# Three edits to a graph-and-experts kernel: how sources are counted, how in-degrees are turned, and which expert results are put by

## The chip, the cores and the metric

The kernel runs on one core of a Trainium2 chip. Its engines are TensorE (PE in the profile, with PEld for its weight loads), VectorE (DVE), ScalarE (ACT), GpSimd (POOL) and SyncE (SP, which here issues transfers only). Each engine works through its own queue in order; semaphores tie them together. Transfers run on 16 DMA engines, whichever engine issued them. The metric is the device time of one execution in microseconds. Nine runs of the kernel before have a median of 1886.43 us (1877.25 to 1897.92).

## The reference

6250 nodes with 256 features, 106,250 directed edges sorted by destination, and eight experts of which each node uses two:

```python
x = x + gnn(layernorm(x), src, dst, W, b)
x = x + ffn(layernorm(x), Wr, br, ln_g, ln_b, W1, b1, W2, b2)

def gnn(f, src, dst, W, b):
    out_deg, in_deg = segment_sum(ones, src), segment_sum(ones, dst)
    msg = (f @ W)[src] * rsqrt(max(out_deg, 1))[src][:, None]
    return relu(segment_sum(msg, dst) * rsqrt(max(in_deg, 1))[:, None] + b)

def ffn(x, ...):
    top_p, top_idx = top_k(softmax(x @ Wr + br), 2)
    weights = top_p / top_p.sum(-1)
    h = gelu((norm(x) * ln_g[e] + ln_b[e]) @ W1[e] + b1[e])    # for each expert e
    y = h @ W2[e] + b2[e]
    return (weights * y of the two chosen experts).sum()
```

Out-degrees are needed before any message can be scaled; in-degrees only when a node's sum is complete.

## The kernel before

**First stage: counting and scaling (about the first 147 us).** The nodes' rows sit in `xres` as 49 tiles of 128. The out-degree of every node is counted by matmuls: a node's number is split into two digits (`digits`, L357), the low one of 7 bits (128 values) and the high one of 49 values. The 106,250 sources lie as 128 rows of 831 columns; `counts` (L367) takes them in 26 chunks of 32 columns. For each chunk DVE makes two one-hot blocks, `oh_hi` (49 x 32, L370) and `oh_lo` (128 x 32, L375), by comparing the digits with counting patterns that GpSimd wrote (`steps_of`, L317 and L318), and PE runs one matmul for each column (L381, 831 in all) that adds into the PSUM tile `hist` (128 x 49), so that node t x 128 + p stands at row p, column t. The blocks have two buffers each. Meanwhile ACT sums the rows and their squares (L465, L475) and copies the turned lists of sources and destinations (L400), which PE turns (L397) behind the chunks of the count that are ahead of it in its queue. The degrees (L515), then scale and shift, multiply the rows of `xres`, which go out to a table `ytab`. The first 42 messages are gathered from x itself and scaled by the degrees of their own sources, for which the digits of those 42 columns are taken too (L408) and turned into one-hots (L415 to L427).

**Second stage: gathers.** A loop over 831 chunks of 128 edges (L1345). For each, POOL issues one indirect DMA (`gather`, L1262), 24 chunks ahead of its use, which fetches 128 rows from `ytab`, or from chunk 168 on from `ptab`, the same table as three bf16 parts. PE multiplies the messages by a one-hot of the destinations (L1372, or the three matmuls L1375 to L1377) into `pm`. The 257th column of a message is 1, so the last column of `pm` counts in-degrees. After a batch of 14 chunks `finish` (L731) turns the sums by PE, two blocks of 128 features with transposes (L741) and the degree column with a matmul by the identity that repeats it over 128 rows (L742), and DVE adds all three blocks into a window of `ring` (L747). When a tile of 128 nodes is complete, `tile_sums` (L773) multiplies it by W (L781), turns its degrees back into a column with a matmul against a one (L785), and finishes the rows; these are stored to the output (L807), and `route_group` sends the normalized rows, sorted by expert, to a table `xs` (POOL scatters, L965).

**Expert steps.** One step takes 256 rows (128 in the first eight steps) of one expert: SyncE loads the rows `xin` and the expert's weights `w` (L1131, L1136; 2182 KB, two buffers), PE turns the rows (L1144), multiplies by W1 (L1201) and W2 (L1220), ACT applies gelu (L1210), and DVE adds the bias and multiplies by the gate into `yo` (L1231, L1237), which has three buffers. The result is added to the output by POOL with two indirect DMAs that accumulate (`add_up`, L1093, line L1095 in the profile). The two adds of one step may overlap (`declare_no_dep`); adds of different steps write the same output and wait for one another. Steps run among the chunks of the second stage as soon as an expert has rows enough, and the remaining ones after the last chunk: the tail.

**Results put by.** While the gathers run (`deferring`, until the loop reaches chunk 807), every third full step is not added to the output at once: `put_by` (L1173) stores its `yo` to a table `ys` by SyncE during the next step, which also frees the buffer. At the end of the gathers `take_back` (L1104) loads them again, up to four at a time, into message buffers, and `add_back` (L1114) adds one step's result to the output, twice in the last chunks and then once in 16 turns of the tail's loop ("beats", L1407 to L1425; about 17 beats are one step, and there are 281 in all):

```python
if sb == SB and deferring[0] and done[0] % 3 == 0:
    stores.append((yo, to_i))
```

**Order.** The program fixes the order of PE, DVE, ACT and SP by hand throughout, and that of POOL until chunk 807; from there on POOL's instructions are placed by the scheduler.

Of the kernel before, what the change touches and what calls it, by code (L numbers as in the profile page):

```python
# [18 lines left out]
P = 128  # L19
# [4 lines left out]
def gnn_then_moe(  # L24
# [12 lines left out]
    nc = tc.nc  # L37
    N, D = x.shape
    NE = src.shape[0]
    E = wr.shape[1]  # L40
    KD = D // P
# [4 lines left out]
    NT = -(-N // P)  # L46
# [18 lines left out]
    WIN = P  # L65
# [5 lines left out]
    GC = 32  # L71
    LO = P
    NHI = NT
    NCP = -(-NCH // GC) * GC
    MW = D + 4
    NMSG = 42
# [4 lines left out]
    SB = TB // P  # L81
# [35 lines left out]
    for g in range(len(GS) - 1):  # L117
        n = P * sum(GS[: g + 1])
# [7 lines left out]
    n = P * sum(GS[:-1])  # L126
# [110 lines left out]
    with tc.manual_schedule(), tc.tile_pool(  # L237
        name="hl", bufs=1
    ) as hl, tc.tile_pool(
        name="rows", bufs=1  # L240
# [7 lines left out]
        flat = hl.tile([P, NCP], I32, name="src_flat")  # L248
        lo = hl.tile([P, NCP], BF16, name="src_lo")
        hi = hl.tile([P, NCP], BF16, name="src_hi")  # L250
        iota_lo = hl.tile([P, LO, GC], BF16, name="iota_lo")
        iota_hi = hl.tile([P, NHI, GC], BF16, name="iota_hi")
        zeros = const.tile([P, SB * XW], F32, name="zeros")
        if FULL < NCP:
            nc.vector.memset(flat[:, FULL:NCP], NPAD - 1)
# [61 lines left out]
        steps_of(iota_hi, [[1, NHI], [0, GC]])  # L317
        steps_of(iota_lo, [[1, LO], [0, GC]])  # L318
        ident = const.tile([P, P], F32, name="ident")
        make_identity(nc, ident)  # L320
        pcol = const.tile([P, 1], F32, name="pcol")
        steps_of(pcol, [[0, 1]], 0, 1)
        steps_of(iota_w, [[1, WIN]])
        for i in range(NMSG):
            nc.gpsimd.memset(msg[i][:, D : D + 1], 1.0)
        after = const.tile([P, P], F32, name="after")
# [27 lines left out]
                in_offset=bass.IndirectOffsetOnAxis(ap=firstT[:, i : i + 1], axis=0),  # L354
            )

        def digits(v, lo, hi, n):  # L357
            for op, by, to in ((ALU.bitwise_and, LO - 1, lo), (ALU.logical_shift_right, 7, hi)):
                part = rows.tile([P, NCP], I32, tag="part", name="part")[:, :n]
                nc.vector.tensor_scalar(part, v, by, None, op0=op)  # L360
                nc.vector.tensor_copy(to, part)

        digits(flat, lo, hi, NCP)
        hist = s1h.tile([P, NT], F32, name="hist")
        chunks = iter(starts)

        def counts(m):  # L367
            for _, c0 in zip(range(m), chunks):
                oh_hi = s1o.tile([P, NHI, GC], BF16, tag="oh_hi", name="oh_hi")
                nc.vector.tensor_tensor(  # L370
                    oh_hi, iota_hi,
                    hi[:, None, c0 : c0 + GC].to_broadcast([P, NHI, GC]), ALU.is_equal,
                )
                oh_lo = s1o.tile([P, LO, GC], BF16, tag="oh_lo", name="oh_lo")
                nc.vector.tensor_tensor(  # L375
                    oh_lo, iota_lo,
                    lo[:, None, c0 : c0 + GC].to_broadcast([P, LO, GC]), ALU.is_equal,
                )
                n = min(GC, NCH - c0)
                for c in range(n):  # L380
                    nc.tensor.matmul(  # L381
                        hist, oh_lo[:, :, c], oh_hi[:, :, c],
                        start=(c0 + c == 0), stop=(c0 + c == NCH - 1),
                    )
# [23 lines left out]
        digits(firstT, lo_e, hi_e, NMSG)  # L408
        loT = rows.tile([P, NMSG, P], BF16, name="loT")
        ohe_hi = rows.tile([P, NMSG, NHI], BF16, name="ohe_hi")  # L410
        nc.vector.tensor_tensor(
            ohe_hi, iota_w[:, None, :NHI].to_broadcast([P, NMSG, NHI]),
            hi_e[:, :, None].to_broadcast([P, NMSG, NHI]), ALU.is_equal,
        )
        for c0 in range(0, NMSG, GC):  # L415
            n = min(GC, NMSG - c0)
            oh_lo = s1o.tile([P, LO, GC], BF16, tag="oh_lo", name="oh_lo")
            nc.vector.tensor_tensor(
                oh_lo[:, :, :n], iota_lo[:, :, :n],
                lo_e[:, None, c0 : c0 + n].to_broadcast([P, LO, n]), ALU.is_equal,  # L420
            )
# [90 lines left out]
        nc.vector.tensor_scalar(sqs, sqs, 1.0 / D, None, op0=ALU.mult)  # L512
        rs0 = rsqrt(rows, sqs, NT, "rs0", EPS)
        deg = rows.tile([P, NT], F32, name="deg")
        nc.vector.tensor_scalar(deg, hist, 1.0, None, op0=ALU.max)  # L515
        both = rows.tile([P, 2, NT], F32, name="both")
        scale0, shift0 = both[:, 0, :], both[:, 1, :]
        nc.vector.tensor_tensor(scale0, rsqrt(rows, deg, NT, "ns"), rs0, ALU.mult)
# [212 lines left out]
    def finish(b, pm):  # L731

        s = seg(b)
        ag = s3.tile([P, D + 1], F32, tag="ag", name="ag")
        nc.scalar.copy(ag, pm)
        if b and seg(b - 1) < s:
            nc.vector.tensor_copy(ring[s][:, :, :OVER], ring[s - 1][:, :, SEGN:])
        yield 0.0, 2
        pt = psum()[:, : (KD + 1) * P].rearrange("p (k q) -> p k q", q=P)
        for k in range(KD):  # L740
            nc.tensor.transpose(pt[:, k, :], ag[:, k * P : (k + 1) * P], ident)  # L741
        nc.tensor.matmul(  # L742
            pt[:, KD, :], ag[:, D : D + 1].to_broadcast([P, P]), ident,
            start=True, stop=True,
        )
        w = register(mybir.EngineType.DVE, win_i[0:1, b : b + 1], RING - WIN)
        nc.vector.tensor_tensor(  # L747
            ring[s][:, :, bass.ds(w, WIN)], ring[s][:, :, bass.ds(w, WIN)], pt, ALU.add
        )
        for t in range(NT):  # L750
            if CLOSE[t] == b:
                side.append([now[0] + 2, 1, tile_sums(t, ring[s], t * P - SEGN * s)])
        yield 0.7, 1
# [19 lines left out]
    def tile_sums(t, sums, c0):  # L773

        g, i = place[t]
        if i == 0:
            held[g] = s3.tile([P, GMAX, 2], F32, tag="mv1", name="mv1")
        x2, mv1 = x_of[t], held[g]
        pw = psum()
        for k in range(KD):  # L780
            nc.tensor.matmul(  # L781
                pw[:, :D], sums[:, k, c0 : c0 + P], gw_sb[:, k, :],
                start=(k == 0), stop=(k == KD - 1),
            )
# [338 lines left out]
    def expert_steps(todo, forever):  # L1123
# [58 lines left out]
        while True:  # L1182
# [224 lines left out]
    while side or todo or batches or not pace["idle"]:  # L1407
        now[0] += 1
        run_side(1.2)
        if batches:  # L1410
            batch = batches.pop(0)
            if batch[0] == len(GS) - 1:
                final = batch
                todo.extend((batch, n) for n in range(PARTS[0]))
            else:
                todo.extend((batch, n) for n in range(STEPS[batch[0]]))
        run_steps(0.9)
        for _, one in rows_out + sums_out:
# [76 lines left out]
```

## Time and profile before

| | |
|---|---|
| median of 9 runs | 1886.43 us |
| profiled execution, its own time | 1898.08 us |
| its span, first to last instruction | 1896.4 us |
| granted TensorE clock, mean | 0.874 |
| PE busy | 1438.2 us (76%) |
| POOL busy | 1147.8 us (61%) |
| DVE busy | 874.8 us (46%) |
| ACT busy | 393.8 us (21%) |
| last gather issued / last result written by DVE / last instruction | 1575.0 / 1882.9 / 1885.4 us |
| `hist` matmuls L381 | 831, 85.4 us busy |
| scatter-adds from `yo` / from `msgs` (results put by) | 86 / 18 |
| stores to `ys` | 9 of 256 KB |

How to read it: the span is cut by stage, since shares over the whole of it mix limits. "Idle before, releaser" tells how long an engine stood idle ahead of a group of instructions and what ended most of that; an engine's idle time costs nothing unless the engine is the one that others wait for. POOL's busy time for an indirect DMA is the time it takes to write its descriptors; the data lands later. Between the last instruction and the end of the span the last add lands and the program closes.

### The profile page before, as it was taken

How to read it: one execution, taken by the hardware profiler on the slowest of the kernel's cores; microseconds unless marked ns; L12 is line 12 of the kernel's file. 1: busy time of each engine (PE TensorE's matmuls, PEld its weight loads, DVE VectorE, ACT ScalarE, POOL GpSimd, SP SyncE). 2: the span in 40 equal slices, each digit the busy share in tenths (PEclk: the TensorE clock that was granted, in tenths of full speed). 3: DMA queues.
4: the chain of work that ended last, by engine and by line, in shares of the span. 5: the costliest groups of instructions: out<-in, count | busy, mean ns of one | idle time of the engine just before them, and what ended most of it. 6: DMA issues, size and time to landing. Idle time of an engine off the chain costs nothing. (4 is left out here: it accounts for less than half of the span.)

```text
span 1896.4 us, 23690 instructions
## 1 busy us (share of the span) xinstructions
PE 1438.2 (76%) x7890; PEld 1171.4 (62%) x7890; DVE 874.8 (46%) x3123; ACT 393.8 (21%) x978; POOL 1147.8 (61%) x1127
## 2 busy tenths in 40 slices
PE   6964645556666797777778878787799699799996
PEld 5863533445555676655556657566577587678886
DVE  8992555425244273444524535426246354722211
ACT  3661211002011120210202112112112112322221
POOL 8847756466757667576666666765766573432321
PEclk9997767678778898898788889898899899899999
DMA  7736756277566776667567577666677576586773
GB/s 223 267 118 231 230 163 192 84 268 241 181 210 202 271 231 209 215 185 231 176 223 207 183 237 222 219 213 197 206 234 253 169 239 204 153 250 188 206 214 72
DMA packets 146583, 389.50 MB, mean 205 GB/s; under 512 B 22316, under 2 KB 89364, under 8 KB 139282
## 3 DMA queue, kind: packets, MB, share of 16 engines
q0 software_dynamic: 70176, 179.11, 34.2%
q1 hardware_dynamic: 76218, 208.73, 31.0%
q8 instruction: 66, 1.08, 0.2%
q14 instruction: 67, 0.55, 0.1%
q10 hardware_dynamic: 56, 0.02, 0.0%
HBM read 324.26 MB, written 63.52 MB: 204 GB/s over the span
## 5 line engine op out<-in xcount | busy, mean ns | idle before, releaser
L1271 POOL DMA_INDIRECT msgs<-ptab,srcT x663 | 649.6, 980 | 332.1 <-issue 131.4
L1201 PE MATMUL ph<-xeT,w 128*128 128x256 f32 (+1 forms) x1792 | 466.0, 398 | 125.0 <-issue 70.3
L1201 PEld LDWEIGHTS ph<-xeT,w 128*128 128x128 f32 x1792 | 339.0, 211 | 176.8 <-issue 79.6
L1220 PE MATMUL py<-w,hT 128*128 128x256 f32 x1664 | 428.3, 392 | 10.9 <-issue 9.3
L1210 ACT ACTIVATE hT<-ph,w 128x256 f32<-128x256 f32 (+1 forms) x448 | 179.8, 455 | 845.8 <-PE ph L1201 371.1
L1220 PEld LDWEIGHTS py<-w,hT 128*128 128x128 f32 x1664 | 304.4, 197 | 47.4 <-issue 11.4
L1095 POOL DMA_INDIRECT out_x<-yo,to_all x86 | 137.7, 1601 | 187.2 <-DVE yo L1237 50.5
L1375 PE MATMUL pm<-msgs,oh 128*128 128x257 bf16 x663 | 193.0, 291 | 4.4 <-issue 4.4
L1376 PE MATMUL pm<-msgs,oh 128*128 128x256 bf16 x663 | 191.6, 289 | 6.0 <-issue 5.9
L1377 PE MATMUL pm<-msgs,oh 128*128 128x256 bf16 x663 | 190.9, 288 | 4.7 <-issue 4.5
L1149 DVE TENSOR_SCALAR xeT<-ptf,w 128x256 f32<-128x256 f32 (+1 forms) x112 | 53.5, 520 | 301.5 <-PE ptf L1144 123.9
L1271 POOL DMA_INDIRECT msgs<-ytab,srcT x126 | 125.7, 998 | 57.9 <-issue 29.1
L747 DVE TENSOR_TENSOR ring<-ring,misc 128x384 f32 x60 | 33.2, 554 | 253.4 <-PE pm L1377 85.4
L223 DVE TENSOR_TENSOR oh<-iota_w,relT 128x896 bf16<-128x896 f32 (+2 forms) x119 | 128.0, 1080 | 24.5 <-remote 10.6
L965 POOL DMA_INDIRECT xs<-rowt,pos_i x98 | 100.8, 1029 | 61.3 <-issue 47.2
L781 PE MATMUL misc<-gw_sb,ring 128*128 128x256 f32 x196 | 64.7, 460 | 74.3 <-DVE ring L747 37.5
L1376 PEld LDWEIGHTS <-oh 128*128 128x128 bf16 x663 | 69.0, 104 | 73.1 <-issue 17.3
L1372 PE MATMUL pm<-msgs,oh 128*128 128x257 f32 x336 | 101.8, 458 | 9.4 <-PEq L576 4.3
L781 PEld LDWEIGHTS misc<-gw_sb,ring 128*128 128x128 f32 x196 | 39.5, 223 | 88.3 <-DVE ring L747 41.4
L381 PE MATMUL hist<-oh_hi,oh_lo 128*128 128x49 bf16 x831 | 85.4, 279 | 11.3 <-DVE oh_lo L375 10.8
L381 PEld LDWEIGHTS <-oh_lo 128*128 128x128 bf16 x831 | 82.4, 150 | 14.2 <-DVE oh_lo L375 13.5
L1372 PEld LDWEIGHTS pm<-msgs,oh 128*128 128x128 f32 x336 | 74.9, 234 | 22.5 <-ACTq L576 4.4
(600 smaller groups left out, 1590.4 us busy)
## 6 DMA issues: line engine op xcount, KB each, us to landing
w<-in_wcat SPq DMA_DIRECT2D x56, 2182.0 KB
xin<-xs SPq DMA_DIRECT2D x48, 260.0 KB
msgs<-ptab,srcT POOLq DMA_INDIRECT x663
strayT<-zeros SPq DMA_DIRECT2D x1, 9216.0 KB
ptab<-part SPq DMA_DIRECT2D x24, 384.0 KB
ytab<-xres SPq DMA_DIRECT2D x7, 896.0 KB
ring<-strayT SPq DMA_DIRECT2D x4, 1536.0 KB
x<-in_x SPq DMA_DIRECT2D x48, 128.0 KB
```

Source lines behind the costliest of these rows:

```text
L223: nc.vector.tensor_tensor(oh[:, :n, :], iota_w[:, None, :].to_broadcast([P, n, WIN]), relT[:, c : c + n, None].to_broadcast([P, n, WIN]), ...
L381: nc.tensor.matmul(hist, oh_lo[:, :, c], oh_hi[:, :, c], start=(c0 + c == 0), stop=(c0 + c == NCH - 1),)
L781: nc.tensor.matmul(pw[:, :D], sums[:, k, c0 : c0 + P], gw_sb[:, k, :], start=(k == 0), stop=(k == KD - 1),)
L1095: ad = nc.gpsimd.indirect_dma_start(out=out, out_offset=bass.IndirectOffsetOnAxis(ap=to, axis=0), in_=rows, in_offset=None, compute_op=ALU ...
L1201: nc.tensor.matmul(ph[:, c - c0, :tb], w[:, k * H + c * P : k * H + (c + 1) * P], xeT[:, k, :tb], start=(k == 0), stop=(k == KD - 1),)
L1210: nc.scalar.activation(hT[:, c, :tb], ph[:, c - c0, :tb], AF.Gelu, bias=w[:, OB1 + c : OB1 + c + 1],)
L1220: nc.tensor.matmul(py[:, s, :], hT[:, c, s * P : (s + 1) * P], w[:, OW2 + c * D : OW2 + (c + 1) * D], start=(c == 0), stop=(c == HC - 1),)
L1271: nc.gpsimd.indirect_dma_start(out=to, out_offset=None, in_=table, in_offset=bass.IndirectOffsetOnAxis(ap=srcT[:, c : c + 1], axis=0),)
L1372: nc.tensor.matmul(pm, oh, msg[i % NMSG][:, : D + 1], start=first, stop=last)
L1375: nc.tensor.matmul(pm, oh, part[:, PW - D : PW + 1], start=first, stop=False)
L1376: nc.tensor.matmul(pm[:, :D], oh, part[:, D : PW - D], start=False, stop=False)
L1377: nc.tensor.matmul(pm[:, :D], oh, part[:, :D], start=False, stop=last)
```

## The change

Three edits. (1) The source count splits a node's number into a low digit of 6 bits (64 values) and a high one of 98. The one-hot blocks become 64 x 32 and 98 x 32, `hist` becomes 64 x 98, and two DVE instructions bring it back to 128 x 49. The 42 early columns keep 7 bits and get a counting pattern of their own, `iota_e`, in blocks of 16 columns. (2) In `finish` the degree column is turned with a transpose into one row in place of 128 equal ones, and DVE's add is split into one for the features (128 rows) and one for that row; in `tile_sums` a transpose takes the place of the matmul by a one. (3) While edges are gathered, the results of two full steps in three are put by, in place of one in three, and in the tail's loop one is added back in 14 beats in place of 16.

```diff
+    CLO, CHI = P // 2, 2 * NT
+    GE = GC // 2
...
-        iota_lo = hl.tile([P, LO, GC], BF16, name="iota_lo")
-        iota_hi = hl.tile([P, NHI, GC], BF16, name="iota_hi")
+        iota_lo = hl.tile([P, CLO, GC], BF16, name="iota_lo")
+        iota_hi = hl.tile([P, CHI, GC], BF16, name="iota_hi")
+        iota_e = hl.tile([P, LO, GE], BF16, name="iota_e")
...
+        steps_of(iota_e, [[1, LO], [0, GE]])
...
-        digits(flat, lo, hi, NCP)
-        hist = s1h.tile([P, NT], F32, name="hist")
+        digits(flat, lo, hi, NCP, CLO)
+        hist = s1h.tile([CLO, CHI], F32, name="hist")
...
-                oh_hi = s1o.tile([P, NHI, GC], BF16, tag="oh_hi", name="oh_hi")
+                oh_hi = s1o.tile([P, CHI, GC], BF16, tag="oh_hi", name="oh_hi")
...
-                oh_lo = s1o.tile([P, LO, GC], BF16, tag="oh_lo", name="oh_lo")
+                oh_lo = s1o.tile([P, CLO, GC], BF16, tag="oh_lo", name="oh_lo")
...
-        for c0 in range(0, NMSG, GC):
-            n = min(GC, NMSG - c0)
-            oh_lo = s1o.tile([P, LO, GC], BF16, tag="oh_lo", name="oh_lo")
+        for c0 in range(0, NMSG, GE):
+            n = min(GE, NMSG - c0)
+            oh_lo = s1o.tile([P, LO, GE], BF16, tag="oh_lo", name="oh_lo")
...
-        nc.vector.tensor_scalar(deg, hist, 1.0, None, op0=ALU.max)
+        for h in range(2):
+            nc.vector.tensor_scalar(
+                deg[h * CLO : (h + 1) * CLO, :], hist[:, h:CHI:2], 1.0, None, op0=ALU.max
+            )
...
-        nc.tensor.matmul(
-            pt[:, KD, :], ag[:, D : D + 1].to_broadcast([P, P]), ident,
-            start=True, stop=True,
-        )
+        nc.tensor.transpose(pt[0:1, KD, :], ag[:, D : D + 1], ident)
...
-        nc.vector.tensor_tensor(
-            ring[s][:, :, bass.ds(w, WIN)], ring[s][:, :, bass.ds(w, WIN)], pt, ALU.add
-        )
+        for rows, ks in ((P, slice(0, KD)), (1, slice(KD, KD + 1))):
+            place_of = ring[s][:rows, ks, bass.ds(w, WIN)]
+            nc.vector.tensor_tensor(place_of, place_of, pt[:rows, ks, :], ALU.add)
...
-        nc.tensor.matmul(
-            pw[:, D : D + 1], sums[0:1, KD, c0 : c0 + P], ones[0:1, 0:1],
-            start=True, stop=True,
+        nc.tensor.transpose(
+            pw[:, D : D + 1], sums[0:1, KD, c0 : c0 + P], ident[0:1, 0:1]
         )
...
-            if sb == SB and deferring[0] and done[0] % 3 == 0:
+            if sb == SB and deferring[0] and done[0] % 3:
                 stores.append((yo, to_i))
...
-        if beat % 16 == 8:
+        if beat % 14 == 6:
             add_back()
```

More of the change, by code (lines that the diff above doesn't have):

```diff
@@ L315, in steps_of @@
                            allow_small_or_imprecise_dtypes=True)
-        steps_of(iota_hi, [[1, NHI], [0, GC]])
-        steps_of(iota_lo, [[1, LO], [0, GC]])
+        steps_of(iota_hi, [[1, CHI], [0, GC]])
+        steps_of(iota_lo, [[1, CLO], [0, GC]])
         ident = const.tile([P, P], F32, name="ident")
@@ L355, in gnn_then_moe, with digits @@
             )
-        def digits(v, lo, hi, n):
-            for op, by, to in ((ALU.bitwise_and, LO - 1, lo), (ALU.logical_shift_right, 7, hi)):
+        def digits(v, lo, hi, n, base):
+            for op, by, to in (
+                (ALU.bitwise_and, base - 1, lo),
+                (ALU.logical_shift_right, base.bit_length() - 1, hi),
+            ):
                 part = rows.tile([P, NCP], I32, tag="part", name="part")[:, :n]
@@ L368, in counts @@
             for _, c0 in zip(range(m), chunks):
-                oh_hi = s1o.tile([P, NHI, GC], BF16, tag="oh_hi", name="oh_hi")
+                oh_hi = s1o.tile([P, CHI, GC], BF16, tag="oh_hi", name="oh_hi")
                 nc.vector.tensor_tensor(
                     oh_hi, iota_hi,
-                    hi[:, None, c0 : c0 + GC].to_broadcast([P, NHI, GC]), ALU.is_equal,
+                    hi[:, None, c0 : c0 + GC].to_broadcast([P, CHI, GC]), ALU.is_equal,
                 )
-                oh_lo = s1o.tile([P, LO, GC], BF16, tag="oh_lo", name="oh_lo")
+                oh_lo = s1o.tile([P, CLO, GC], BF16, tag="oh_lo", name="oh_lo")
                 nc.vector.tensor_tensor(
                     oh_lo, iota_lo,
-                    lo[:, None, c0 : c0 + GC].to_broadcast([P, LO, GC]), ALU.is_equal,
+                    lo[:, None, c0 : c0 + GC].to_broadcast([P, CLO, GC]), ALU.is_equal,
                 )
@@ L407, in gnn_then_moe @@
         hi_e = rows.tile([P, NMSG], F32, name="hi_e")
-        digits(firstT, lo_e, hi_e, NMSG)
+        digits(firstT, lo_e, hi_e, NMSG, LO)
         loT = rows.tile([P, NMSG, P], BF16, name="loT")
@@ L414, in gnn_then_moe @@
         )
-        for c0 in range(0, NMSG, GC):
-            n = min(GC, NMSG - c0)
-            oh_lo = s1o.tile([P, LO, GC], BF16, tag="oh_lo", name="oh_lo")
+        for c0 in range(0, NMSG, GE):
+            n = min(GE, NMSG - c0)
+            oh_lo = s1o.tile([P, LO, GE], BF16, tag="oh_lo", name="oh_lo")
             nc.vector.tensor_tensor(
-                oh_lo[:, :, :n], iota_lo[:, :, :n],
+                oh_lo[:, :, :n], iota_e[:, :, :n],
                 lo_e[:, None, c0 : c0 + n].to_broadcast([P, LO, n]), ALU.is_equal,
```

## The prediction

> **What bounds the kernel now.** I read the windows of time first, to tell the stages apart, then the groups of instructions, then the timelines of GpSimd (POOL) and SyncE in the last stage and of PE, DVE and ACT in the first. The chain of waits was no help: it holds one piece, the last DMA. In a window line the columns are its length, then busy us (and instructions) of PE, weight load, DVE, ACT and POOL, the granted clock, the DMA share and GB/s.
>
> ```profile
> 1200.00:1300.00 100.00, 79.65 (x430) 61.92 (x429) 36.68 (x123) 14.01 (x33) 67.05 (x66) 0.91 0.67 208
> 1700.00:1800.00 100.00, 100.00 (x479) 88.06 (x478) 21.53 (x70) 23.47 (x56) 31.13 (x21) 1.00 0.69 203
> ```
>
> There are three stages: until about 147 us a first one, in which degrees are counted; the gathers, whose last POOL issue is at 1575 us; then a tail in which PE does nothing but expert steps and is never idle. While edges are gathered, neither PE nor POOL is full, so the next question is who waits for whom.
>
> ```profile
> L1271 POOL DMA_INDIRECT msgs<-ptab,srcT x663 | 649.6, 980 | 332.1 <-issue 131.4
> L1095 POOL DMA_INDIRECT out_x<-yo,to_all x86 | 137.7, 1601 | 187.2 <-DVE yo L1237 50.5
> L1375 PE MATMUL pm<-msgs,oh 128*128 128x257 bf16 x663 | 193.0, 291 | 4.4 <-issue 4.4
> ```
>
> The third line decides: ahead of the 663 matmuls that first touch a gathered message PE idles 4.4 us in all. Messages are never late. The table of waits says the reverse: POOL waits 109.5 us (134 times) for PE to release a message buffer. So POOL's time between 150 and 1575 us is not on the path, PE's order of work is, with its waits on DVE and ACT. The tail looks PE-bound, but its scatter-adds into the output tell another story (POOL's timeline, first add of most pairs, and SyncE's for the same stretch):
>
> ```profile
> 1737.44 1.55 POOL L1095 DMA_INDIRECT out_x<-yo,to_all  x1 [8.34 <-DVE xeT L1149]
> 1739.30 1.55 POOL L1095 DMA_INDIRECT out_x<-yo,to_all  x1 [0.31 <-issue]
> 1743.87 1.55 POOL L1095 DMA_INDIRECT out_x<-msgs,to_all  x1 [3.02 <-issue]
> ...
> 1771.40 1.55 POOL L1095 DMA_INDIRECT out_x<-yo,to_all  x1 [3.04 <-DMA out_x<-msgs,to_all]
> ...
> 1781.22 1.55 POOL L1095 DMA_INDIRECT out_x<-yo,to_all  x1 [6.42 <-DVE gate L1170]
> ...
> 1793.73 1.55 POOL L1095 DMA_INDIRECT out_x<-yo,to_all  x1 [9.11 <-DMA out_x<-yo,to_all]
> ...
> 1799.94 1.55 POOL L1095 DMA_INDIRECT out_x<-yo,to_all  x1 [2.81 <-DMA out_x<-yo,to_all]
> ```
> ```profile
> 1769.39 0.33 SPq L1136 DMA_DIRECT2D w<-in_wcat  x1
> ...
> 1783.65 0.33 SPq L1136 DMA_DIRECT2D w<-in_wcat  x1
> ```
>
> Two adds make a pair, one step's result. A pair starts only when the pair before it has landed. Pair starts run 1737.4, 1743.9, 1752.7, 1765.0, 1771.4, 1781.2, 1793.7, 1799.9, 1809.3, 1822.2, 1828.5: ten distances in 91.1 us, 9.1 us each, in a pattern of about 6.4, 9.4 and 12.6 us, which sums to two steps (weight loads leave SyncE every 14.25 us). The short ones have no weight load behind them; the long ones do, so an add lands late while 2182 KB of weights pass. I write this as **6.4 us for each pair and 4.65 us more for each weight load**: 3 x 6.4 + 2 x 4.65 = 28.5. POOL is busy only 31 of 100 us there, yet this chain of landings has no room: counted back from the last step, the pairs at 1781.2 and 1793.7 carry results that DVE began to write at 1755.1 and 1769.3, some 24 us late. The chain catches up only near 1841, with one pair a step.
>
> **Part 1, put by two of three.** 48 full steps run, 29 of them before results stop being put by (at chunk 807 of 831; the loops' own counts put the 29th at chunk 798 and the 30th at 813). Now 9 go to ys (9 stores in the list of DMAs); then 29 - 9 = 20. Eleven pairs leave the gather stage and come back in the tail.
> What it gives in the gather stage: 22 adds x (1.60 + 0.30 gap) = 42 us of POOL. I take **0** of it, since PE idles 4.4 us for messages; the ends are 0 and 42. What it adds there: 11 stores of 256 KB on SyncE, 0.33 us of issue each, queued behind the next step's weight load and waiting for a result that is done by then; 2.8 MB at 205 GB/s is 14 us of DMA in a stage with a share of 0.6 to 0.75. Hidden by that free share; without it weights come late, up to 14 us.
> In the tail: before, 20 step pairs and 9 put by; after, 19 and 20, so 39. Slots: two at the end of the gathers, then a beat in 14 from 6 on, 18 slots up to beat 244 of 281, so nothing is left over for the drain. From the first slot (1639.5 us, once POOL has sent the last rows to xs) there are 18 put-by pairs and 17 step pairs, and 15 weight loads. The last pair starts 34 x 6.4 + 15 x 4.65 = 287 us after the first. The same count on the kernel before, from 1639.5 to 1841.2, has 20 distances and 13 loads, 188 us, and 9 us in which the chain waited for results: 197, against 201.7 measured. So I add 4 us: 291. Last pair at 1930.5 in place of 1883.5: **+47 us**. The next thing late is DVE's result write: yo has three buffers, released by the adds, so steps are held back and PE idles about 4 us a step (2.2 x 6.4 + 4.65 = 18.7 us of chain, 14.25 us of work). Ends: with no delay by weights at all 34 x 6.4 = 218, ready at 1857, no loss (0); with 9.1 us for each pair 309, +65. Twenty-two more loads of 128 KB from ys use a DMA share of 0.31 that is free.
> The Trainium skill, TensorE: Matmul & The Clock Gate (Part 1), has the clock halve after some 3.4 us of idle PE. The row that bears on it is the window 300 to 400 us, PE busy 45.66 with 0.67 granted, against 1.00 above. By the page each held-back step starts at half clock and would lose an estimated 1.7 us; that lies inside the idle time and alters nothing in my sum.
>
> **Part 2, the source count.**
>
> ```profile
> 109.20 6.40 PE L381 MATMUL hist<-oh_hi,oh_lo 128*128 128x49 bf16 x63 [0.19 <-DVE oh_lo L375]
> ...
> 124.66 2.45 PE L556 MATMUL pk<-part,loT 128*128 128x98 bf16 x28 [0.38 <-DVE part L525]
> ```
> ```profile
> 80.84 0.65 ACT L400 CAST srcT<-ptE 128x240 int32<-128x240 f32 x1 [14.38 <-PE ptE L397]
> ```
> ```profile
> 114.00 1.09 DVE L223 TENSOR_TENSOR oh<-iota_w,relT 128x896 f32<-128x896 f32 x1 [1.76 <-ACT relT L400]
> ```
>
> DVE makes two one-hots a chunk: 2286 ns for 4096 elements, 971 for 1568, so 0.520 ns an element and 155 fixed. After: 2048 and 3136 elements, 1220 + 1787 = 3007 against 3257, 0.25 us less. ACT waits 14.4 us for PE's first turned rows at 80.8, behind 16 chunks, and is then back to back to 114, where DVE waits for it. So only the 16 chunks count: 4.0 us, about 1.2 for DVE's short waits on PE (0.2 to 0.4 each), 1.0 for a shorter last chunk on PE, less 0.2 for a second DVE pass over the histogram: **-6 us**, between -3 and -9. GpSimd's iotas: 1673 + 4169 ns become 3.2 + 2.15, and 2.15 more ahead of 42 gathers; POOL waits 23.2 us for DVE later, which hides it. The edges' one-hots cost 0.2 us more.
> On PE a chunk's matmul, now 128 weight columns and 49 moving, both strided, goes every 99 ns ((6.40 - 0.28) / 62). After: 64 and 98. The nearest row, L556 with 128 contiguous weight columns and 98 moving, goes every 81 ns. Below: 50 ns, when weights alone count. Above: 198, when strided moving columns alone count. DVE allows 94 (3007 / 32). I take 81, so PE stays out of the way.
> The skill's same page (Weight-path perf modes) speaks against the edit: fast weight load asks for all 128 columns, so 64 lose it. Its plain rate would give an estimated 53 ns, still under 94, and the same sum.
>
> **Part 3, degrees turned as one row.**
>
> ```profile
> 273.37 0.39 PE L742 MATMUL misc<-ident,ag 128*128 128x128 f32 x2
> 273.59 1.03 PE L1372 MATMUL pm<-msgs,oh 128*128 128x257 f32 x4
> ```
>
> A fp32 matmul is two records, 0.22 us together here; a transpose (L741, 120 records for 120) is one. So 0.11 us goes for each of 60 batches and about 0.13 (L785, 98 records) for each of 49 tiles: 13 us of PE, 15 at the mean clock of 0.874. DVE's add (554 ns for 384 columns) becomes two. L1231 costs 684 ns for 512 columns and 418 for 256, so 1.04 a column and 152 fixed: 418 + 285 = 703, 9 us more over 60, of which PE sees 12 x 0.15 = 2 us (its waits on ring, 37.5 us, 12 times). PE is 80% busy there and its other waits stay. I take **-5 us**; ends -15 and +9.
>
> **The sum.** 1896.4 + 47 - 6 - 5 = 1932 us of span. The median, 1886.4, lies 10 below the profiled execution's span, so 1886.4 + 36 = **1922 us**; the ends of the costs give 1895 to 1952 as this case's own range.
>
> **Rivals.** (a) *The tail takes the adds for nothing.* For it: POOL is 31% busy there. Then only parts 2 and 3 count: 1875. Against it: a weight load would have to delay the chain by 1.5 us or less in place of 4.65, and pairs were late before. (b) *POOL paces the gathers.* Its 42 us come off as well and the adds fit: 1833. Against it: the 4.4 us. (c) *PE takes over the count.* At 198 ns a chunk costs 6.3 us in place of 3.3, so 26 x 3.0 = 79 us more, 6 less gained: 1922 + 85 = 2007. Against it: the 81 ns row; it decides above 94 ns. (d) *The chain is freer than I think*, at 2.2 us a weight load: the last pair starts at 1639.5 - 11 + 218 + 4 + 33 = 1883.5 as before, so 1886.
>
> **Chances.** Forecast 0.74, (a) 0.10, (b) 0.04, (c) 0.05, (d) 0.07. 0.5% is what measurements of this kernel tell from no change: faster than 1877 is most of (a) and (b), 0.13; within, (d) and an edge of (a), 0.10; slower 0.77. The range takes in (a): 1872 to 1952.
>
> **What would show it.** Right: in the tail, pairs back to back with no idle longer than the landing of the one before, about 39 of them, PE under 85% busy from 1650 on, DVE waiting for DMA out_x ahead of yo. The last gather some 11 us earlier. L381 closer than 94 ns, no PE wait charged to DVE's L747 beyond 2 us more. Wrong: PE full in the tail and the last result not after 1883 us, or the gather stage shorter by 20 us or more, or DVE waiting for PE hist in each chunk.

## The result, and the profile after

The changed kernel takes 1985.64 us (median of 20 runs, 1971.38 to 2001.47) against 1887.6 us for the kernel before in the same runs (62 runs): a ratio of 1.052, interval 1.0499 to 1.0541. It is slower by 5.2%, 98 us, where 36 us were forecast. The profiled execution after has a span of 1987.9 us and a mean granted clock of 0.864.

Three marks cut both spans into stages: the first gather of an edge chunk by POOL, the last message matmul, and the end.

| us | before | after | difference |
|---|---|---|---|
| start to first gather | 149.3 | 203.6 | +54.3 |
| first gather to last message matmul | 1467.3 | 1450.9 | -16.4 |
| last message matmul to the end | 279.7 | 333.4 | +53.7 |

**The first stage.** PE's timeline and ACT's (start, duration, engine and line, idle before):

```profile
99.75 13.19 PE L389 MATMUL hist<-oh_hi,oh_lo 128*64 128x98 bf16 x76
112.87 0.46 PE L405 MATMUL ptE<-ident,src_rows 120*128 120x120 f32 x1
```
```profile
113.57 0.62 ACT L408 CAST srcT<-ptE 128x240 int32<-128x240 f32 x1 [40.99 <-PE ptE L405]
...
119.85 0.62 ACT L408 CAST srcT<-ptE 128x240 int32<-128x240 f32 x1 [1.48 <-PE ptE L405]
...
126.05 0.62 ACT L408 CAST srcT<-ptE 128x240 int32<-128x240 f32 x1 [1.41 <-PE ptE L405]
```

A run of 76 count matmuls takes 13.19 us, so one follows another every (13.19 - 0.34) / 75 = 171 ns; before it was 99. ACT's first turned list of sources, at 80.84 us before, comes at 113.57. The 16 chunks ahead of it account for that: each takes PE 32 x 171 ns = 5.47 us, where DVE's 3.26 paced them before, and 16 x 2.2 = 35 us. Then ACT waits for PE again ahead of every copy, where before it ran back to back. DVE, which paced the count before, now waits for it (groups of DVE between 10 and 180 us, the first line before, the others after):

```profile
L370 DVE TENSOR_TENSOR oh_hi<-iota_hi,src_hi 128x1568 bf16<-128x1568 bf16 x26 | 25.3, 971 | 3.4 <-PE hist L381 3.1
L378 DVE TENSOR_TENSOR oh_hi<-iota_hi,src_hi 128x3136 bf16<-128x3136 bf16 x26 | 46.6, 1791 | 63.8 <-PE hist L389 41.8 <-remote 16.7 <-issue 5.2
L383 DVE TENSOR_TENSOR oh_lo<-iota_lo,src_lo 128x2048 bf16<-128x2048 bf16 x26 | 31.8, 1222 | 0.0
```

The one-hots themselves cost what was foreseen (1791 + 1222 = 3013 ns a chunk; 3007 forecast). The 41.8 us of waiting for PE stand where 3.1 stood.

**The gathers.** Window of time (PE, weight load, DVE, ACT, POOL busy; clock; DMA share; GB/s), and rows of the page after; the last line is from the table of waits before:

```profile
1200.00:1300.00 100.00, 76.43 (x411) 59.48 (x409) 46.16 (x195) 17.68 (x41) 62.15 (x62) 0.88 0.64 208
```
```profile
L1278 POOL DMA_INDIRECT msgs<-ptab,srcT x663 | 646.9, 976 | 366.1 <-PE pm L1384 148.3
...
L1382 PE MATMUL pm<-msgs,oh 128*128 128x257 bf16 x663 | 191.9, 289 | 5.3 <-issue 5.2
...
L1102 POOL DMA_INDIRECT out_x<-yo,to_all x64 | 100.8, 1575 | 153.2 <-DMA out_x<-msgs,to_all 60.8
...
POOL msgs L1271 <- PE pm L1377: 109.5, 134, 4.1
```

22 adds left this stage (86 from `yo` became 64). PE still idles only 5.3 us ahead of the first matmul on a message, and POOL waits longer for PE than before: 148.3 us in place of 109.5.

**The tail.** POOL's timeline, the first add of each pair; PE by windows; SyncE's weight loads; DVE's longest wait after 1650 us (total, times, longest):

```profile
1746.41 1.55 POOL L1102 DMA_INDIRECT out_x<-msgs,to_all  x1 [9.01 <-issue]
...
1752.85 1.57 POOL L1102 DMA_INDIRECT out_x<-yo,to_all  x1 [3.04 <-DMA out_x<-msgs,to_all]
...
1762.92 1.55 POOL L1102 DMA_INDIRECT out_x<-msgs,to_all  x1 [6.64 <-issue]
...
1775.18 1.55 POOL L1102 DMA_INDIRECT out_x<-yo,to_all  x1 [8.77 <-DMA out_x<-msgs,to_all]
```
```profile
1700.00:1800.00 100.00, 96.70 (x445) 84.22 (x446) 22.99 (x81) 23.30 (x56) 34.37 (x24) 0.97 0.80 240
1800.00:1900.00 100.00, 93.87 (x437) 81.57 (x436) 17.05 (x58) 20.28 (x49) 32.05 (x21) 0.97 0.68 196
1900.00:1988.00 88.00, 31.97 (x138) 26.70 (x136) 7.53 (x25) 6.71 (x16) 36.20 (x24) 0.69 0.40 62
```
```profile
1850.25 0.34 SPq L1143 DMA_DIRECT2D w<-in_wcat  x1
...
1870.05 0.34 SPq L1143 DMA_DIRECT2D w<-in_wcat  x1
...
1888.53 0.33 SPq L1143 DMA_DIRECT2D w<-in_wcat  x1
...
1907.80 0.33 SPq L1143 DMA_DIRECT2D w<-in_wcat  x1
```
```profile
DVE yo L1244 <- DMA out_x<-yo,to_all: 92.2, 7, 16.9
```

Distances of 6.4, 10.1 and 12.3 us, as before, but the chain of adds no longer catches up: it runs on until 1975.05, where the last pair starts. DVE waits 92.2 us in seven pieces for a result buffer that an add still reads, weight loads then leave SyncE every 18.5 to 19.8 us in place of 14.25, and PE, 94% to 97% busy until 1900, is busy 32 of the last 88 us.

### The profile page after: what moved, and what is told of

The parts are those of the page before. It is cut to its first block, busy times and chain, and to the rows that moved or that the text cites. A ratio compares the mean times of both kernels' runs of the same rounds, so it can differ in the third digit from the quotient of the medians.

```text
span 1987.9 us, 23636 instructions
## 1 busy us (share of the span) xinstructions
PE 1488.2 (75%) x7781; PEld 1215.7 (61%) x7781; DVE 868.0 (44%) x3185; ACT 394.8 (20%) x978; POOL 1121.1 (56%) x1128
## 5 line engine op out<-in xcount | busy, mean ns | idle before, releaser
L1278 POOL DMA_INDIRECT msgs<-ptab,srcT x663 | 646.9, 976 | 366.1 <-PE pm L1384 148.3
L1102 POOL DMA_INDIRECT out_x<-yo,to_all x64 | 100.8, 1575 | 153.2 <-DMA out_x<-msgs,to_all 60.8
L389 PE MATMUL hist<-oh_hi,oh_lo 128*64 128x98 bf16 x831 | 146.0, 349 | 8.7 <-issue 4.7
L757 DVE TENSOR_TENSOR ring<-ring,misc 128x256 f32 x120 | 36.5, 345 | 257.9 <-remote 150.0
L389 PEld LDWEIGHTS <-oh_lo 128*64 128x64 bf16 x831 | 141.2, 192 | 12.8 <-issue 8.4
L1379 PE MATMUL pm<-msgs,oh 128*128 128x257 f32 x336 | 106.5, 473 | 21.0 <-issue 10.0
L1102 POOL DMA_INDIRECT out_x<-msgs,to_all x40 | 62.2, 1554 | 103.4 <-issue 63.9
```

The source lines that it names most:

```text
L389: nc.tensor.matmul(hist, oh_lo[:, :, c], oh_hi[:, :, c], start=(c0 + c == 0), stop=(c0 + c == NCH - 1),)
L1102: ad = nc.gpsimd.indirect_dma_start(out=out, out_offset=bass.IndirectOffsetOnAxis(ap=to, axis=0), in_=rows, in_offset=None, compute_op=ALU ...
L1278: nc.gpsimd.indirect_dma_start(out=to, out_offset=None, in_=table, in_offset=bass.IndirectOffsetOnAxis(ap=srcT[:, c : c + 1], axis=0),)
L1379: nc.tensor.matmul(pm, oh, msg[i % NMSG][:, : D + 1], start=first, stop=last)
```

## The experiments

The chips differ: the kernel before takes 1710 us on one, 1887 to 1911 on others. Every ratio is against the kernel before on the same chip; stage lengths of different chips are not mixed without saying so.

### The three parts alone (before at 1710.1 us)

e1 changes only two lines of before:

```diff
-            if sb == SB and deferring[0] and done[0] % 3 == 0:
+            if sb == SB and deferring[0] and done[0] % 3:
-        if beat % 16 == 8:
+        if beat % 14 == 6:
```

> Part 1 alone (two results of three put by, one added back in 14 beats). Theory, the chain of landings: the tail holds 39 pairs in place of 28 or 29, so from the last gathered matmul to the end it takes about 334 us (280 before), and the gathers are unchanged: total about 1887 + 47 to 54 = 1934 to 1941, ratio 1.025 to 1.029. Rival, POOL paces the gathers: the gathers are some 16 us shorter, as in the changed kernel, total 1918 to 1925, ratio 1.017 to 1.020. Rival, the tail grew only since everything before it came later: ratio 1.00.

e2 has the count of 64 x 98 alone (all of the diff that touches `CLO`, `CHI`, `GE`, `digits` and `hist`):

> Part 2 alone (6-bit digits, 98 values). Theory, strided moving columns cost 1.74 ns each, so 98 of them 170 ns a matmul and PE takes over the count: first gather at about 203 us in place of 149, all else as before, total about 1887 + 54 = 1941, ratio 1.029. Rival, the later stages win part of it back because the zero fill and other transfers of the first stage are over by then: ratio under 1.02.

e3 has the transposes and the divided add in `finish` and `tile_sums` alone:

> Part 3 alone (degrees turned as one row). Theory A, it is this part that made the gathers 16 us shorter in the changed kernel's profile: total about 1872, ratio 0.99. Theory B, PE saves 13 us of work that its other waits take back, DVE pays 9 us: total 1880 to 1889, ratio 0.996 to 1.001. Rival, the longer way over DVE decides: ratio above 1.003.

| kernel | ratio (interval) | start to first gather, us | first gather to last message matmul | last message matmul to the end |
|---|---|---|---|---|
| e1, part 1 | 1.0106 (1.0048 to 1.0165) | 149.1 | 1239.6 | 337.9 |
| e2, part 2 | 1.0292 (1.0248 to 1.0335) | 199.4 | 1275.8 | 283.0 |
| e3, part 3 | 1.0006 (0.9982 to 1.0030) | 149.3 | 1279.8 | 289.2 |

Part 2 costs 50 us, all ahead of the first gather. Part 3 does nothing that can be measured. Part 1 takes 36 to 40 us off the gathers and adds 49 to 55 to the tail, if e2 and e3 stand in for the kernel before, which has no profile on this chip; its median is 17 us longer. None of the three ranges forecast for e1 had this: the tail grew as its theory said, and the gathers shrank by more than twice the 16 us of its rival. On this chip PE does wait for messages, as e1's page shows, and for rows of `xs` that POOL scattered (tables of waits, e1's line first, then two of e3):

```profile
L1375 PE MATMUL pm<-msgs,oh 128*128 128x257 bf16 x663 | 187.3, 283 | 25.1 <-DMA msgs<-ptab,srcT 25.1
```
```profile
PE ptf L1144 <- DMA xin<-xs: 63.3, 6, 22.7
...
PE ptf L1140 <- DMA xin<-xs: 101.6, 9, 23.7
...
PE pm L1371 <- DMA msgs<-ptab,srcT: 15.0, 9, 4.1
```

The wait for messages is not shorter in e1; the wait for rows of `xs` is, by 38 us, as much as the stage gained. So how much POOL's time is worth seems to depend on the chip. On the chip of the first profiles the same row has 4.4 us and no DMA behind it.

Both whole kernels were run again where before takes 1909.1 us:

> The kernel before once more, for a profile on the chip of this call. Theory: on a chip where the kernel takes about 1710 us, messages reach PE with little time to spare (a few us, not 28), PE waits for rows that POOL scattered to xs, and the gathers take about 1279 us from the first gather to the last batch. Rival: the gathers take 1243 us here as in the run of part 1 alone, so that part 1 gave nothing.

> The changed kernel once more, beside it on the same chip. On a chip where before takes 1710 us, the single parts gave +1.1, +2.9 and +0.1%: the sum is 1.040 to 1.045. On the chip of the first comparison it is 1.052. If the parts work on one another, the ratio is outside these.

e5 has a span of 1912.4 us, e6 2004.1, with a ratio of 1.0461 (1.0423 to 1.0499). First gather 149.3 and 209.1; from there to the last message matmul 1484.7 and 1457.2; tail 278.5 and 337.7. The three differences (+60, -27, +59) have the signs and the order of those above. The single parts add up to 1.040 on the chip of 1710 us, where the whole gives 1.046 here and 1.052 in the first comparison. A smaller gain in the gathers would account for that, but part 1 alone was not run on a slower chip.

### What sets the distance of two count matmuls

e4 exchanges the operands of part 2 (98 columns as weights, 64 moving):

```diff
-                        hist, oh_lo[:, :, c], oh_hi[:, :, c],
+                        hist, oh_hi[:, :, c], oh_lo[:, :, c],
```

> Part 2 with the operands of the count's matmul exchanged: 98 weight columns and 64 moving ones, hist is 98 x 64 and turned once by PE before the degrees. Theory, the moving operand's strided columns set the interval at 1.74 ns each: 64 x 1.74 = 111 ns a matmul in place of 167 to 174, a chunk 3.6 us, first gather at about 155 to 160 us, total about 1895, ratio 1.003 to 1.006. Rival, the weights set it since fewer than 128 columns lose the fast load: 98 weight columns take longer than 64, interval 170 ns or more, ratio 1.03 or more.

```profile
69.66 14.68 PE L389 MATMUL hist<-oh_lo,oh_hi 128*98 128x64 bf16 x87
```

It came out at 167 ns a matmul, not 111 (ratio 1.027, 1.0229 to 1.031), so moving columns alone don't decide. e7 keeps 128 weights and takes 98 moving values, half of which never occur; e8 makes two matmuls of 64 x 49 for each column in place of one of 128 x 49:

```diff
-        iota_hi = hl.tile([P, NHI, GC], BF16, name="iota_hi")
+        iota_hi = hl.tile([P, CHI, GC], BF16, name="iota_hi")
```
```diff
+                    for h in range(2):
-                            hist, oh_lo[:, :, c], oh_hi[:, :, c],
+                            hist[64 * h : 64 * h + 64, :], oh_lo[:, 64 * h : 64 * h + 64, c],
+                            oh_hi[:, :, c],
```

> The count with a low digit of 7 bits (128 weight columns) and 98 high values (half of them unused for a given low digit), so that the matmul has 128 weight columns and 98 moving, all strided as before. Theory S, fast loading of 128 weight columns was lost and loading and streaming add up: 33 + 102 = 135 ns a matmul within a chunk. Rival M, the moving columns alone set it: 170 ns. Rival O, loads hide behind streaming: about 100 ns. DVE takes 4.07 us a chunk, so the first gather comes at about 170 us whichever holds, unless PE takes more than 127 ns.

> The count of before with each matmul made in two halves of 64 weight columns (1662 matmuls of 64 weight columns and 49 moving, strided). Theory S: 67 + 51 = 117 ns each. Rival M, moving columns alone: 85 ns each. Rival F, any load of fewer than 128 columns has a fixed price: 167 ns each.

```profile
69.70 14.54 PE L382 MATMUL hist<-oh_hi,oh_lo 128*128 128x98 bf16 x80
```
```profile
69.72 7.41 PE L382 MATMUL hist<-oh_hi,oh_lo 128*64 128x49 bf16 x113
```

With all 128 weight columns and 98 moving e7 has (14.54 - 0.36) / 79 = 179 ns, as slow as the change (one run 1971.8 us). That is near the 170 which the moving side alone gives. The width of the weights is not the cause: with a fast load there is no gain. Together with e4, a column costs 1.7 ns on either side: 49 moving at least 85 ns, 98 on either side 167. What both have in common with the kernel before, and L556 (81 ns for 98 columns) has not, is that neighbouring columns lie 64 bytes apart (`oh[:, :, c]` steps over 32 bf16). e8's matmuls come every 63 ns on average here, 127 a pair, which none of its expectations had. The starts in the trace say more: in seven stretches of 4 to 33 pairs the two halves of a pair start 4 ns apart, and one pair follows another every 110 ns, which is what a single load of 64 such columns sets below. So the halves seem to pass side by side rather than one faster than the other; outside these stretches the starts are spread, at a median of 122 ns a pair, for which no run shows the reason.

e9 lays the 98 values side by side, e10 both operands, e12 the 49 values of the kernel before:

```diff
-                oh_hi = s1o.tile([P, CHI, GC], BF16, tag="oh_hi", name="oh_hi")
+                oh_hi = s1o.tile([P, GC, CHI], BF16, tag="oh_hi", name="oh_hi")
-                        hist, oh_lo[:, :, c], oh_hi[:, :, c],
+                        hist, oh_lo[:, :, c], oh_hi[:, c, :],
```

> Part 2 alone (64 x 98), with the one-hot of the 98 values laid out value by value, so that the 98 moving columns of one matmul lie side by side instead of 64 bytes apart; the 64 weight columns stay 64 bytes apart. So far: 128 weights and 49 moving 85-104 ns, 64 and 98 166-174, 98 and 64 166-167, 128 and 98 167-187, all with 64 bytes between columns. Theory S (the stride sets it): a column 64 bytes apart costs 1.7 ns (85/49 and 167/98), a side-by-side one 0.83 ns (81/98, L556), load and stream overlap and the longer one sets the interval: load 64 x 1.7 = 109, stream 81, so 109 ns. Theory F (the fast load is lost below 128 columns, and load and stream add): 168 ns as before, whatever the layout. Theory D (VectorE, which makes the one-hots, sets it): the interval follows its busy time per chunk, and the matmuls wait for DVE.

> As e9_hi_rows, and the 64 weight columns side by side too. Theory S: load 64 x 0.83 = 53, stream 81: 81 ns a matmul, the figure of the prediction, and the first gather back near before's 149 us unless VectorE's writes in the new layout take longer. Theory F: 168 ns.

> Before, with the one-hot of its 49 values laid out value by value: 128 weight columns 64 bytes apart, loaded fast, and 49 moving columns side by side. Theory S: the stream falls from 85 ns to 41, the interval to what the fast load of 128 strided columns takes (below 85; 128 x 1.7 / 4 = 54), so VectorE's 80 us of one-hots set the count and the first gather comes 5 to 20 us earlier: ratio 0.990 to 0.998. If VectorE writes the new layout more slowly, the count grows instead and the matmuls wait for DVE. Theory F: no change of the interval.

PE's timelines of e9, e10 and e12 (32 columns are a chunk):

```profile
74.73 3.78 PE L389 MATMUL hist<-oh_hi,oh_lo 128*64 128x98 bf16 x32 [0.69 <-DVE oh_lo L383]
```
```profile
74.30 2.82 PE L389 MATMUL hist<-oh_hi,oh_lo 128*64 128x98 bf16 x32 [2.71 <-DVE oh_lo L383]
```
```profile
70.75 2.21 PE L381 MATMUL hist<-oh_hi,oh_lo 128*128 128x49 bf16 x32 [1.64 <-DVE oh_lo L375]
```

| kernel | weight columns | moving columns | ns between matmuls, median | longer of the two by 1.7 or 0.83 ns a column |
|---|---|---|---|---|
| L556 before | 128 together | 98 together | 81 | 81 (stream) |
| e10 | 64 together | 98 together | 81 | 81 (stream) |
| e9 | 64 apart | 98 together | 110 | 109 (load) |
| after | 64 apart | 98 apart | 167 to 173 | 167 (stream) |
| e4 | 98 apart | 64 apart | 167 | 167 (load) |
| e7 | 128 apart | 98 apart | 181 | 167 (stream) |
| before | 128 apart | 49 apart | 100 (every eighth 85) | 83 (stream) |
| e12 | 128 apart | 49 together | 63 | load, see below |
| e8, a pair | 64 apart, twice | 49 apart, twice | 122 (110 in the regular stretches) | 109 (load), if the halves pass side by side |

Load and stream overlap and the longer one sets the distance. A moving column 64 bytes from its neighbour costs twice one that lies beside it (167 against 81 ns for 98). On the load side 64 columns take 110 ns apart and at most 81 together (e10), where the stream sets the pace; what they cost there by themselves no run shows. e9's 110 and e10's 81 were forecast to 1 ns; the theory by which load and stream add (168 in both) is out. The rows of 100 and 181 lie 14 to 17 above it and are not explained.

Two sentences of the Trainium skill bear on this. SBUF — State Buffer (Door 1: The DMA port swizzle) has lines of 16 bytes, so that a bf16 operand may step by 8 elements for free and pays for every access to a new line beyond that; the step here is 32 elements. If that penalty is what the rows show, its price, which the page leaves out, is 1.7 ns in place of 0.83 for a moving column; no run here tries a step between 1 and 32 elements on the count. TensorE: Matmul & The Clock Gate (Weight-path perf modes) gives fast weight load to 128 columns alone, and the rows agree: 128 columns 64 bytes apart load in no more than 63 ns (e12), 64 of them take 110 (e9).

None of the three is a gain: VectorE pays for the order. Groups of DVE in e10, to be held against 1791 and 1222 ns above:

```profile
L378 DVE TENSOR_TENSOR oh_hi<-iota_hi,src_hi 128x3136 bf16<-128x3136 bf16 x26 | 88.7, 3411 | 0.1
L383 DVE TENSOR_TENSOR oh_lo<-iota_lo,src_lo 128x2048 bf16<-128x2048 bf16 x26 | 59.3, 2281 | 0.0
```

The same values written side by side take 1.9 times as long, and PE waits for DVE in each chunk. The first gather comes at 177.3 (e9), 205.0 (e10) and 163.4 us (e12). e12 is slower than before, 1.007 (1.0034 to 1.0106), though its count takes the least time on PE for each column of sources (63 ns).

### What putting by costs the tail

e11 is e1 with an `add_back` that returns at once, so that the put-by results are missing from its output. e13, e14 and e15 put by two of five, every second, and none:

```diff
-            if sb == SB and deferring[0] and done[0] % 3 == 0:
+            if sb == SB and deferring[0] and done[0] % 5 in (2, 4):
```
```diff
+            if sb == SB and deferring[0] and done[0] % 2 == 0:
```
```diff
+            if sb == SB and deferring[0] and done[0] < 0:
```

> Part 1 alone (two of three put by), without the last steps' adding of the put-by results: the 20 pairs of adds of put-by results are left out, so these rows of the output lack those results. Theory G (the prediction's, with its upper end for the gathers): the tail falls back to before's length, 280-290 us, since it is the 20 pairs x 6.4 us less before's put-by pairs that lengthened it, while the gather stage keeps its gain (about -40 us on a chip like that of e1_part1, -15 to -28 on a slow one): time of before less 20 to 50 us. Rival (the tail is set by something else, PE's work or the weight loads): the tail stays over 320 us and the time near part 1's own ratio, 1.01.

> Before, with two of five results put by during the gathers (12 pairs kept, where before keeps 9 and the change 20). Theory H (the tail has a floor of some 277 us, which PE's own work sets, and pairs past the room under it cost 6.4 us each; 333 with 20 pairs, so about 11 are free): tail 277-285 us, last message matmul 4 us earlier than before's on a slow chip (3/11 of 16) and 11 on a fast one: ratio 0.994 to 1.001. Theory L (each pair costs the same from the first one on, 53.6/11 = 4.9 us): tail +15, ratio 1.002 to 1.006.

> Before, with every second result put by (14 pairs kept). Theory H: three pairs past the room, tail about 295-300 us; gathers 7 us shorter on a slow chip, 18 on a fast one: ratio 0.998 to 1.007. Theory L: tail 280 + 5 x 4.9 = 305, ratio 1.003 to 1.010.

> Before, with no result put by. Theory H: tail stays at its floor, about 277 us, since 9 pairs fit under it; gathers longer by 9/11 of what part 1 takes off them: 13 us on a slow chip, 31 on a fast one: ratio 1.004 to 1.018. Theory L: tail 280 - 9 x 4.9 = 236, ratio 0.983 to 0.992.

| pairs added back | kernel | ratio (interval) | tail, us |
|---|---|---|---|
| 0 of 20 put by | e11 | 0.9933 (0.9901 to 0.9966) | 277.2 |
| 0 | e15 | 1.0197 (1.0170 to 1.0225) | 278.6 |
| 9 | before, e5 | 1 | 279.7, 278.5 |
| 12 | e13 | 1.0028 (1.0008 to 1.0049) | 281.5 |
| 14 | e14 | 1.0110 (1.0069 to 1.0152) | 290.8 |
| 20 | e1, after, e6 | (1.0106 for e1) | 337.9, 333.4, 337.7 |

e11's median is 10 us below the kernel before, not the 20 to 50 that were forecast, but its tail falls back. The tail has a floor of 277 to 280 us, in which PE is full (e11):

```profile
1700.00:1800.00 100.00, 100.00 (x479) 88.06 (x478) 20.89 (x70) 23.51 (x56) 21.63 (x14) 1.00 0.69 216
```

Up to about 12 pairs fit under it; from 14 to 20 each costs (333.4 to 337.9 - 290.8) / 6 = 7.1 to 7.9 us. A price from the first pair on would have given e15 a tail of 236 us and is out. The ratios of e13, e14 and e15 lie just above theory H's ranges (1.001, 1.007 and 1.018 at most), with intervals that reach into them: the gathers seem to gain less from more pairs put by, and to lose more with none, than its shares of pairs say. e14's tail, at 290.8, is shorter than the 295 to 300 forecast. Of the shares tried (none, two of five, a half, two of three) none beats one of three, and no kernel of this study that adds all its results beats the one before.

### What putting by saves in the gathers

e16 repeats e11. In e17 each add that was put by has an iota in its place; e18 stores every put-by result twice more:

```diff
                 stores.append((yo, to_i))
+                for _ in range(sb):
+                    sums_out.append((now[0] + BEHIND, partial(
+                        nc.gpsimd.iota, filler, pattern=[[1, 1536]], base=0, ...
```
```diff
                 nc.sync.dma_start(ys[n], yo)
+                for more in ys2:
+                    nc.sync.dma_start(more[n], yo)
```

> e11_no_addback again (20 pairs put by and not added: their results are left out of these rows), as the measure for the two that follow on the same chip: gathers 15 to 40 us shorter than before's, tail 277 us.

> e16 with 40 GpSimd iotas of 1536 elements (about 1.64 us each by 1673 ns for 1568 elements) in the places, in the gathers, of the 40 adds that were put by; nothing reads what they write, and the put-by results are left out as in e16. Theory P (an add's time on GpSimd is what the gathers save): the gather stage grows by some 40 x 1.9 = 76 us, to the length it has with no result put by (e15: 1516 us from first gather to last message matmul on a slow chip), time of e16 plus 50 to 76. Theory M (it is not POOL's time but the add's own landing, waits or traffic): no change, within 10 us of e16.

> e16 with each of the 20 put-by results stored three times in place of once, the second and third to memory that nothing reads (40 x 128 KB more by SyncE's queue, as many bytes as the 40 adds write); the put-by results are left out as in e16. Theory P: within 10 us of e16. Theory M by traffic: the gathers grow by 20 us or more.

Medians 1878.0, 1889.8 and 1885.3 us, with before at 1889.4 on that chip: ratios 0.9945 (0.9914 to 0.9976), 0.9992 (0.9965 to 1.002) and 0.9983 (0.995 to 1.0015). The tails stay at 277 to 279 us, so the differences are the gathers'. Twenty pairs put by in place of nine are worth 11 us here (10 in e11). Forty iotas, 57 us of POOL in e17's trace, cost 12 us again, not 50 to 76; the extra stores cost 7, not 20, and 7 is within the scatter of these runs. Neither theory holds as it was put: theory P had the stores right and the iotas wrong, theory M missed both, the iotas by little. POOL's time counts, at about a fifth of its length on this chip; that traffic counts is not shown. The single profiles of e11 and e16, the same kernel on two chips, differ by 17 us in this stage (1449.2 and 1431.9), so profiles can't tell the shares apart further. Why e15 loses 37 us for 18 adds more (34 us of POOL), where 22 fewer gain 11, stays open.

## Why the prediction was wrong

**Part 2, 81 ns a matmul: this step failed.** It took the nearest row by the number of columns, L556, and set aside that L556's operands lie together and the count's don't. The nearest row by layout was the count itself, 99 ns for 49 columns, and its end of the bounds, 198 for 98 moving columns alone, was the right side: 167 to 173 measured. With 171 a chunk takes 5.47 us in place of 3.26, and 26 chunks 57 us more, close to the 58 by which the last count matmul came later (115.6 before, 173.8 after). So part 2 is +54 where -6 stood, and with it alone put right the sum is 1922 + 60 = 1982 against 1985.64. That this comes so close is in part luck: the tail cost 7 us more than its term and the gathers 10 to 16 less than theirs. The range was also narrower than its own terms: their stated ends add up to 1820 to 1957 us, or 1971 with the 14 us of late weights, and the measured time lies above that as well. Rival (c), PE takes over the count, is what happened, though at 171 ns and not at the 198 for which it gave 2007 us; it had 0.05 and was left outside the range. Its point of decision, 94 ns, and its sign, DVE waiting for PE in the chunks, were right. The dismissal of the lost fast load did no harm, but by luck: 64 columns as they lie here took 110 ns (e9), not the estimated 53, and 110 is above the 94 that DVE allows. In the changed kernel that load only hides behind the longer stream.

**Part 1 in the tail, +47: right in mechanism and near in size.** The chain of pairs began at 1670.8, not 1639.5: 31 us later, where the later start less the shorter gathers would give 38. From there it had 34 distances with 15 weight loads, as counted, and took 304 us in place of 291, up to the last pair at 1975.05. The tail grew by 53.7; past the room a pair costs 7.1 to 7.9 us, its share of the loads among it. DVE's wait for the result buffers came as forecast, and steps 18.5 to 19.8 us apart for the 18.7 that were worked out. What the count didn't show is the room itself, about 12 pairs that PE's own work hides.

**Part 1 in the gathers, 0: too low, between its ends.** The two profiles gave 16 us of the 42, in a stage in which profiles scatter by as much; the medians of e11 and e16 gave 10 and 11, and the chip of 1710 us 36 to 40. "PE idles 4.4 us for messages" shows that no message was late, not that POOL's time is free: e17's iotas pass through at a fifth.

**Part 3, -5: 0 measured** (1.0006, 0.9982 to 1.0030), inside its ends. The matmuls are gone from the profile (one record where there were two), and the saved time is not on the path.

Rival (a) and (d) fell with e1: the tail does not take 20 pairs. Rival (b) was nearly true of the gathers on the chip of 1710 us, where part 1 gains 36 to 40 of its 42 us, and loses them in the tail all the same.

## What to carry to other kernels

Price a matmul from a row with the same layout of its operands, not only with the same count of columns: here 64 bytes between moving columns cost a factor of two, and halving one digit while doubling the other moved the count from 99 to 171 ns, because the longer side sets the pace. When two engines are within 3% of each other (99 ns on PE, 3257 / 32 = 102 on DVE), any edit that makes one cheaper has to be priced on the other, and its bad bound belongs in the range. Work put off into a stage that an engine fills is free up to the room beside that engine's work, and then costs its whole chain: find the room by putting off none, some and most.

## What was not expected of the hardware

Chips differ by 12% for one and the same kernel (1710 to 1911 us), in the granted clock of the gathers (0.88 to 0.90 in e1 to e4, 0.84 to 0.86 in the profiles of the other chips) and in what PE waits for. What makes them differ is open. One-hots written with the compared value repeated along the innermost dimension take 1.9 times as long on VectorE (3411 in place of 1791 ns for 3136 elements). Two matmuls on 64 weight columns each, into the two halves of one tile, start 4 ns apart in parts of e8's trace, with 110 ns from pair to pair, the distance that one load of 64 such columns sets by itself (e9).
